# Turning the fourth layer's features on SyncE's DMA queue and its rows on GpSimd's, with buffers of their own

## The chip, the cores and the metric

The kernel runs on one core of a Trainium2 chip. The metric is the device time of one execution in microseconds (us). TensorE (PE in the profile) does the matmuls, VectorE (DVE), ScalarE (ACT) and GpSimd (POOL) the elementwise work, and DMA engines move data between the core's memory and HBM. DMAs are issued from the instruction queues of SyncE (SP) and GpSimd here; each of these queues is worked off in its order, so a DMA whose semaphore is not yet there holds up all that stand behind it.

## The reference

A graph of N = 4096 nodes with 256 features each passes through four attention layers over the same adjacency matrix. After every layer the result is added to the layer's input and each row is normalised. The third and the fourth layer are what matters here; cut to that:

```python
# layer 2: additive attention, one head
h = x @ W
e = leaky_relu((h @ a[:D])[:, None] + (h @ a[D:])[None, :], 0.01)
att = softmax(where(adj > 0, e, -1e12), axis=1)
x = layernorm(x + elu(att @ h))
# layer 3: cosine attention
Qn = (x @ Wq.T) / max(norm(x @ Wq.T, axis=-1), 1e-4)
Kn = (x @ Wk.T) / max(norm(x @ Wk.T, axis=-1), 1e-4)
att = softmax(where(adj > 0, Kn @ Qn.T, -9e15), axis=1)
x = layernorm(x + 0.5 * (att @ x) + 0.5 * x)
```

Layers are counted from 0 in the code: the "fourth layer" of this document is layer 3 of the reference. Before its attention can begin, all of its Q and K have to be there, projected from the features that layer 2 leaves behind, normalised by row and turned so that the 128 projected values lie on the partitions.

## The kernel before, in words

Nodes are worked in NB = 8 blocks of 512 rows; a block is attended against NT = 32 tiles (j = 0 to 31) of 128 nodes. The features X stay in the core's memory throughout.

**Layer 2** (`additive_one`) walks the units (b, j). For each unit ACT writes e (L451), DVE multiplies it by the edges' mask into prob (L453, three buffers), and PE adds prob times V to the block's sums (L459). The masks, one DMA of 512 KB for two tiles, are issued from SP's queue (L449, four buffers). When block b has been summed, DVE divides (L465, L467), and in the first tiles of block b + 1 it finishes block b: `add_elu`, then `layernorm_block`. So the finished features of block b are there early in block b + 1.

**The preparation of layer 3** (`Cosine.prepare`) is laid between the tiles of layer 2's last block, for the blocks n = 0 to 5; the blocks 6 and 7 are prepared inside layer 3. It has three steps for each block:

- step 0 turns the features: `block_apart` lets DVE transpose X in squares of 32 x 32 into a tile `squares` (L130, two instructions), writes it to a tile in HBM (L133, 512 KB) and reads it back in another order into xT (L135, four DMAs of 128 KB). The function `turned_apart` does this.
- step 1 projects: PE multiplies xT with both weight matrices (L852), ACT sums the squares (L857), DVE copies the result to `rows` (L858) and scales it (L863).
- step 2 turns the rows: again `turned_apart`, from `rows` through `squares` and HBM into T (L130, L133, L135).

Step 1 of block n stands behind tile j = 2 + 4n of the last block in PE's order, step 2 at j = 5 + 4n. Layer 3 reads T of block n at its tile j = 4n. Between these steps GpSimd also issues the first masks of layer 3 (L835), each behind a small copy `tick` (L91) that makes it wait for a chosen tile of layer 2.

Only PE's order is written out by hand (`manual_schedule` for PE). The orders of DVE, ACT, POOL and SP come from a scheduler, which puts an instruction where its inputs and its buffers are free. That is why the features of the blocks 0, 1 and 2 are already transposed in the course of layer 2, long before the place where the code names them.

What the steps share in the kernel before: one buffer `squares` (pool `co_once`) for features and rows alike, two buffers of xT and two of rows (pool `co_in`), and one queue for all the DMAs of the turning, GpSimd's for the blocks 0 to 5 (`eng = nc.gpsimd if b < NB - 2 else nc.sync`) and SP's for 6 and 7.

Of the kernel before, what the change touches and what calls it, by code (L numbers as in the profile page):

```python
# [9 lines left out]
FP = mybir.dt.float32  # L10
# [8 lines left out]
P = 128  # L19
D = 256  # L20
KC = D // P
QB = 4
# [6 lines left out]
def kernel(  # L29
# [27 lines left out]
    nc = tc.nc  # L57
# [4 lines left out]
    def pool(stack, name, bufs, **kw):  # L62
        return stack.enter_context(tc.tile_pool(name=name, bufs=bufs, reuse_waits="tile", **kw))
# [56 lines left out]
            copies[c](xT[:, c, :], pt)  # L120
        return xT.rearrange("p c (k i) -> p c k i", i=P)

    def turned_apart(once, dr, part, to, eng):

        B = P // QB
        squares = once.tile([P, QB, KC, P], FP, name="squares")
        for c in range(KC):
            nc.vector.transpose(squares[:, :, c, :].rearrange("p q (k n) -> p k q n", n=B),  # L130
                                part(c).rearrange("p k (q f) -> p k q f", f=B))
        far = dr.tile([QB, B, QB, KC * P], FP, name="squares_far")
        eng.dma_start(far.rearrange("a f q m -> (a f) (q m)"), squares.rearrange("p q c m -> p (q c m)"))  # L133
        for q in range(QB):
            eng.dma_start(to[q * B:(q + 1) * B], far[:, :, q, :].rearrange("a f m -> f a m"))  # L135
        return to.rearrange("p a (c m) -> p c a m", c=KC)
# [264 lines left out]
    def additive_one(w_sb, slope, tail, op, follow):  # L401
# [3 lines left out]
        with ExitStack() as lay:  # L405
# [4 lines left out]
            row = keep.tile([P, N], FP, name="row")  # L410
            zp = pool(lay, "gb_z", 3)
            sb = pool(lay, "gb_sb", 2)
            mp = pool(lay, "gb_mask", 4)
            dr = pool(lay, "gb_dram", 2, space=bass.MemoryType.DRAM)

# [6 lines left out]
                return ps.tile([P, QW], FP, name="g")  # L422

            def turn(b):
                return transposed_block(sb, bank, b)

            def project(b, xT, ks=range(QB)):
                groups = [(k, 1, bank().rearrange("p (n f) -> p n f", n=1)) for k in ks]
# [380 lines left out]
    class Cosine:  # L809
# [7 lines left out]
        def start(self):  # L817
            keep = self.stack.enter_context(tc.tile_pool(name="co_keep", bufs=1, side="right", reuse_waits="tile"))
            self.pool = self.stack.enter_context(tc.tile_pool(name="co_in", bufs=2, side="right", reuse_waits="tile"))
            self.masks = self.stack.enter_context(tc.tile_pool(name="co_mask", bufs=4, side="right", reuse_waits="tile"))  # L820
            self.mask = {}

            self.T = [keep.tile([P, QB, 2 * P], FP, name=f"T{b}") for b in range(NB)]
            self.dram = self.stack.enter_context(tc.tile_pool(name="co_dram", bufs=2, space=bass.MemoryType.DRAM))
            self.once = self.stack.enter_context(tc.tile_pool(name="co_once", bufs=1, side="right", reuse_waits="tile"))
            self.w_sb = keep.tile([P, KC, 2 * P], FP, name="w3_sb")
            load_w(self.w_sb[:, :, :P], wq3T, nc.sync)
            load_w(self.w_sb[:, :, P:], wk3T, nc.sync)
# [8 lines left out]
        def prepare(self, bank, b, step):  # L837

            in_, w_sb = self.pool, self.w_sb

            eng = nc.gpsimd if b < NB - 2 else nc.sync
            if step == 0:
                self.xT[b] = block_apart(in_, self.once, self.dram, b, eng)
            elif step == 1:
                xT = self.xT.pop(b)
                norm = in_.tile([P, QB, 2], FP, name="norm")
                rows = self.rows[b] = in_.tile([P, QB, 2, P], FP, name="rows")
                for k in range(0, QB, 2):
                    pr = bank().rearrange("p (t n f) -> p t n f", t=2, f=P)
                    for t in range(2):  # L850
                        for c in range(KC):
                            nc.tensor.matmul(pr[:, t, :, :], xT[:, c, k + t], w_sb[:, c, :],  # L852
                                             start=(c == 0), stop=(c == KC - 1))
                    for t in range(2):
                        for n in range(2):
                            sq = in_.tile([P, P], FP, name="sq")
                            nc.scalar.activation(sq, pr[:, t, n, :], AF.Square, accum_out=norm[:, k + t, n:n + 1])  # L857
                    nc.vector.tensor_copy(rows[:, k:k + 2], pr)  # L858
                v = in_.tile([P, QB * 2], FP, name="v")
                nc.vector.tensor_scalar_max(v, norm.rearrange("p k n -> p (k n)"), 1e-8)  # L860
                r = inverse_root(v, QB * 2)
                flat = rows.rearrange("p k n f -> p (k n) f")
                nc.vector.tensor_tensor(flat, flat, r.unsqueeze(2).to_broadcast([P, QB * 2, P]), OP.mult)  # L863
            else:
                rows = self.rows.pop(b)
                turned_apart(self.once, self.dram, lambda n: rows[:, :, n, :], self.T[b], eng)

    def cosine_attention(co, tail):
        MJ = co.MJ
        T = [t.rearrange("p k (n i) -> p n k i", n=2) for t in co.T]  # L870
        with ExitStack() as lay:
            sb = pool(lay, "co_sb", 3)
            yp = pool(lay, "co_y", 2)

            pa = pool(lay, "co_pa", 1, space=PSUM)
            pz = pool(lay, "co_pz", 2, space=PSUM)
            ps = pool(lay, "co_ps", 2, space=PSUM)
            ov = out.rearrange("(t p) d -> p t d", p=P)
            acc, prob, y = {}, {}, {}

            def bank():
                return ps.tile([P, QW], FP, name="g")

            def weights(b, j):
                m = b, j // MJ
                if m not in co.mask:
                    co.load_mask(*m)
                p = bank() if b and j % 2 else pz.tile([P, QW], FP, name="p")
                nc.tensor.matmul(p.rearrange("p (k i) -> p k i", k=QB), T[j // QB][:, 0, j % QB], T[b][:, 1],  # L889
                                 start=True, stop=True)  # L890

                z = prob[b, j] = sb.tile([P, QW], FP, name="prob")
                nc.scalar.activation(z, p, AF.Exp)  # L893
                nc.vector.tensor_tensor(z, z, co.mask[m][:, j % MJ, :], OP.mult)  # L894

            def sums(b, js):
                if js[0] == 0:
                    acc[b] = [pa.tile([P, D + 1], FP, name=f"acc{k}") for k in range(QB)]
                for k in range(QB):
                    for j in js:  # L900
                        nc.tensor.matmul(acc[b][k], prob[b, j][:, k * P:(k + 1) * P], X[:, j, :],  # L901
                                         start=(j == 0), stop=(j == NT - 1))

            def outputs(b, n):

                for k0 in range(0, QB, n):
                    mv = fin.tile([P, n, 2], FP, name=f"mv{n}")
                    for k in range(k0, k0 + n):
                        rden = fin.tile([P, 1], FP, name="rden1")
                        nc.vector.reciprocal(rden, acc[b][k][:, D:])  # L910
                        nc.vector.scalar_tensor_tensor(y[b][:, k, :], acc[b][k][:, :D], rden, y[b][:, k, :], OP.mult, OP.add)
                        one_row(mv, k - k0, y[b][:, k, :])
                    normalise([y[b][:, k, :] for k in range(k0, k0 + n)], mv)
                    nc.sync.dma_start(ov[:, b * QB + k0:b * QB + k0 + n, :], y[b][:, k0:k0 + n, :])

            units = [(b, j) for b in range(NB) for j in range(NT)]
            LAG = 2
            steps = {(0, j + n): (NB - 2 + b, step) for b, j in enumerate((1, 12)) for step, n in enumerate((0, 5, 8))}
            for i in range(len(units) + LAG):
                if i < len(units):  # L920
                    b, j = units[i]
                    weights(b, j)
                    if (b, j) == (0, 1):
                        tail(bank)
                    if (b, j) in steps:
                        co.prepare(bank, *steps[b, j])
                if i >= LAG:
                    b, j = units[i - LAG]
                    if j == NT - 8:
                        y[b] = yp.tile([P, QB, D], FP, name="y")  # L930
                        nc.scalar.mul(y[b], X[:, b * QB:(b + 1) * QB, :D], 1.5)

                    if i < len(units):
                        sums(b, [j])
                    elif i > len(units):
                        sums(b, [j - 1, j])
                    if j == NT - 1:
                        outputs(b, QB if b < NB - 1 else 2)
# [88 lines left out]
```

## Time and profile before

| | us |
|---|---|
| median of three runs (2909.53 to 2911.84) | 2911.56 |
| the profiled execution's own time | 2912.43 |
| its span (first to last instruction) | 2910.7 |
| PE busy | 2889.4 |
| DVE busy | 1954.2 |
| ACT busy | 1655.3 |
| POOL busy | 965.2 |

Of the DMAs that turn features and rows, POOL's queue issues 12 writes (L133) and 48 reads (L135), SP's queue 4 and 16. The span is the time that the profile can divide; the execution's own time is 1.73 us longer. In the rows shown below, a line such as "PE L852 MATMUL acc<-w_sb,xT" is an instruction at line 852 that reads w_sb and xT and writes acc; "[7.90 <-DMA xT<-squares_far]" says that its engine sat idle for 7.90 us before it, until that DMA had landed. A float32 matmul shows as two records, so a tile of layer 2 (four matmuls) has 8 and a projection of a block (eight) has 16. In the tables by stretch of time the last columns are the clock granted to PE (1.00 is full), the mean busy share of the DMA engines, and GB/s.

### The profile page before, as it was taken

How to read it: one execution, taken by the hardware profiler on the slowest of the kernel's cores; microseconds unless marked ns; L12 is line 12 of the kernel's file. 1: busy time of each engine (PE TensorE's matmuls, PEld its weight loads, DVE VectorE, ACT ScalarE, POOL GpSimd, SP SyncE). 2: the span in 40 equal slices, each digit the busy share in tenths (PEclk: the TensorE clock that was granted, in tenths of full speed). 3: DMA queues.
4: the chain of work that ended last, by engine and by line, in shares of the span. 5: the costliest groups of instructions: out<-in, count | busy, mean ns of one | idle time of the engine just before them, and what ended most of it. 6: DMA issues, size and time to landing. Idle time of an engine off the chain costs nothing.

```text
span 2910.7 us, 50256 instructions
## 1 busy us (share of the span) xinstructions
PE 2889.4 (99%) x20141; PEld 1553.4 (53%) x20141; DVE 1954.2 (67%) x2541; ACT 1655.3 (57%) x2589; POOL 965.2 (33%) x735
## 2 busy tenths in 40 slices
PE   9999999999999999999999999999998999999998
PEld 4333333333643333333333358888887777777776
DVE  8899999998677777777777765655666423333333
ACT  7899999997356666666666654444443222222222
POOL 0010010100068989989889860000012000000000
PEclk9999999999999999999999999999999999999999
DMA  7566667665068989889889875655566434434341
GB/s 205 103 138 137 139 139 145 135 129 90 1 134 193 185 186 193 183 187 192 182 189 191 182 171 133 178 163 150 154 185 168 87 58 58 58 58 58 58 58 29
DMA packets 214061, 391.72 MB, mean 135 GB/s; under 512 B 16338, under 2 KB 94146, under 8 KB 212931
## 3 DMA queue, kind: packets, MB, share of 16 engines
q0 software_dynamic: 106336, 190.35, 40.2%
q1 hardware_dynamic: 107216, 197.88, 22.3%
q8 instruction: 158, 2.59, 0.3%
q14 instruction: 77, 0.62, 0.1%
q10 hardware_dynamic: 274, 0.26, 0.0%
HBM read 325.46 MB, written 29.43 MB: 122 GB/s over the span
## 4 chain that ended last, share of the span: by engine, by line
PE 98%; DMA 1%; DVE 1%; ACT 0%; issue 0%; POOL 0%; DVEq 0%; POOLq 0%
PE acc L293 23%; PE acc L901 15%; PE acc L678 15%; PE p L645 15%; PE acc L459 8%; PE g L459 7%; PE p L889 4%; PE g L889 3%; PE g L572 2%; PE g L196 1%; PE pv L587 1%; PE acc L196 1%; PE g L118 1%; PE acc L852 1%; DMA squares_far<-squares 1%; PE g L305 0%
## 5 line engine op out<-in xcount | busy, mean ns | idle before, releaser
L657 DVE TENSOR_TENSOR prob<-p,mask 128x1024 f32<-128x1024 f32 x512 | 624.1, 1223 | 209.5 <-ACT p L647 203.8
L647 ACT ACTIVATE p<-p,shift 128x1024 f32<-128x1024 f32 x512 | 556.2, 1088 | 325.2 <-PE p L645 324.4
L293 PE MATMUL acc<-prob,V 128*32 128x512 f32 x6144 | 664.0, 592 | 1.2 <-DVE prob L283 1.2
L664 POOL TENSOR_TENSOR den<-den,prob 128x1024 f32<-128x1024 f32 x248 | 626.9, 2528 | 72.6 <-DVE prob L657 64.7
L280 ACT ACTIVATE prob<-row,dst 128x512 f32<-128x512 f32 x1020 | 633.1, 712 | 0.1
L283 DVE SCALAR_TENSOR_TENSOR prob<-prob,mask 128x2048 f32<-128x2048 f32 x256 | 582.5, 2286 | 24.2 <-ACT prob L280 20.7
L645 PE MATMUL p<-qT,kT 64*64 64x512 f32 x4096 | 532.3, 590 | 0.8 <-DVE prob L657 0.8
L678 PE MATMUL acc<-prob,V 64*64 64x512 f32 x4096 | 531.5, 589 | 0.0
L901 PE MATMUL acc<-X,prob 128*128 128x257 f32 x2048 | 485.5, 380 | 0.0
L901 PEld LDWEIGHTS acc<-X,prob 128*128 128x128 f32 x2048 | 388.6, 190 | 162.8 <-issue 112.9
L894 DVE TENSOR_TENSOR prob<-prob,mask 128x512 f32<-128x512 f32 x256 | 176.2, 690 | 409.3 <-ACT prob L893 408.1
L293 PEld LDWEIGHTS acc<-prob,V 128*32 128x32 f32 x6144 | 197.3, 110 | 453.1 <-issue 433.6
L451 ACT ACTIVATE e<-row,dst 128x512 f32<-128x512 f32 x256 | 184.0, 721 | 241.8 <-DVE prob L453 212.6
L678 PEld LDWEIGHTS acc<-prob,V 64*64 64x64 f32 x4096 | 155.9, 133 | 285.4 <-issue 278.1
L645 PEld LDWEIGHTS p<-qT,kT 64*64 64x64 f32 x4096 | 154.4, 133 | 277.3 <-issue 261.5
L453 DVE SCALAR_TENSOR_TENSOR prob<-e,mask 128x512 f32<-128x512 f32 x256 | 177.6, 695 | 173.4 <-PE acc L459 93.9
L91 POOL COPY tick<-prob 128x1 f32<-128x1 f32 x35 | 40.0, 1144 | 645.9 <-DVE prob L283 644.8
L835 POOL DMA_DIRECT2D mask<-in_adjT x64 | 47.6, 743 | 582.2 <-DVE prob L894 505.3
L670 POOL DMA_DIRECT2D den<-prob x240 | 231.6, 965 | 14.7 <-DVE prob L657 7.5
L893 ACT ACTIVATE prob<-p 128x512 f32<-128x512 f32 x144 | 85.7, 596 | 257.0 <-PE p L889 243.0
L459 PE MATMUL acc<-V,prob 128*128 128x257 f32 x1024 | 225.1, 380 | 0.0
L459 PE MATMUL g<-V,prob 128*128 128x257 f32 x1024 | 224.1, 380 | 0.0
(160 smaller groups left out, 1965.6 us busy)
## 6 DMA issues: line engine op xcount, KB each, us to landing
mask<-in_adjT SPq DMA_DIRECT2D x256, 512.0 KB
den<-prob POOLq DMA_DIRECT2D x240, 512.0 KB, 5.3
mask<-edges SPq DMA_DIRECT2D x256, 128.0 KB
mask<-in_adjT POOLq DMA_DIRECT2D x64, 512.0 KB, 5.7
edges<-in_adj POOLq DMA_DIRECT2D x32, 512.0 KB, 10.0
den<-prob SPq DMA_DIRECT2D x16, 512.0 KB
row<-far SPq DMA_DIRECT2D x7, 1024.0 KB
squares_far<-squares POOLq DMA_DIRECT2D x12, 512.0 KB, 4.0
```

The lines of the kernel that those rows point to most:

```text
L280: nc.scalar.activation(z[:, h, :], r, AF.Relu, bias=-1.0, scale=dst[:, j, h:h + 1])
L283: nc.vector.scalar_tensor_tensor(z, z, 1.0, mask[m][:, j % MJ, :].unsqueeze(1).to_broadcast([P, H, QW]), OP.add, OP.mult)
L293: nc.tensor.matmul(acc[b][h * G:(h + 1) * G, n, :], part, prob[b, j][:, h, :], start=(j == 0), stop=(j == NT - 1))
L459: nc.tensor.matmul(acc[b][k][:, :D + 1], prob[b, j][:, k * P:(k + 1) * P], V[:, j, :], start=(j == 0), stop=(j == NT - 1))
L645: nc.tensor.matmul(p[c * d:(c + 1) * d, r, :], kT[half, c, j * d:(j + 1) * d], qT[half, c, cols], start=True, stop=True)
L647: nc.scalar.activation(p, p, AF.Exp, bias=shift)
L657: nc.vector.tensor_tensor(z, p, mask[m][:, j % MJ, :].unsqueeze(1).to_broadcast([P, KC, QW]), OP.mult)
L664: nc.gpsimd.tensor_tensor(to, to, flat, OP.add)
L670: nc.gpsimd.dma_start(to, flat, accum_op=OP.add)
L678: nc.tensor.matmul(acc[b][c][r * d:(r + 1) * d, :], V[half, j, r * d:(r + 1) * d], prob[b, j][half, r, :], start=(j == 0), stop=(j == NH - 1))
L889: nc.tensor.matmul(p.rearrange("p (k i) -> p k i", k=QB), T[j // QB][:, 0, j % QB], T[b][:, 1], start=True, stop=True)
L901: nc.tensor.matmul(acc[b][k], prob[b, j][:, k * P:(k + 1) * P], X[:, j, :], start=(j == 0), stop=(j == NT - 1))
```

## The change

Features and rows each get what they shared before.

- The features' step gets three pools that live with layer 2 itself (`gb_turn` with three buffers of xT, `gb_squares` with one, `gb_far` in HBM), handed over as `follow.turning`; inside layer 3, for the blocks 6 and 7, it gets `co_turn` (two), `co_squares` and `co_turn_far`. Layer 2's own transposed blocks use `gb_turn` too, instead of two buffers in `gb_sb`.
- The features' DMAs (step 0) are issued from SP's queue for all blocks. The rows' DMAs (step 2) stay on GpSimd's queue for the blocks 0 to 5 and on SP's for 6 and 7.
- The rows keep `co_once` for their squares; `rows` itself moves there too and so has one buffer instead of two.

```diff
-    def turned_apart(once, dr, part, to, eng):
+    def turned_apart(squares, far, part, to, eng):
         B = P // QB
-        squares = once.tile([P, QB, KC, P], FP, name="squares")
+        squares = squares.tile([P, QB, KC, P], FP, name="squares")
+        far = far.tile([QB, B, QB, KC * P], FP, name="far")
         for c in range(KC):
             nc.vector.transpose(...)
-        far = dr.tile([QB, B, QB, KC * P], FP, name="squares_far")
         eng.dma_start(far..., squares...)
         for q in range(QB):
             eng.dma_start(to[q * B:(q + 1) * B], far[:, :, q, :]...)
...
             sb = pool(lay, "gb_sb", 2)
+            xp = pool(lay, "gb_turn", 3)
+            sq = pool(lay, "gb_squares", 1)
+            far = pool(lay, "gb_far", 2, space=bass.MemoryType.DRAM)
+            follow.turning = xp, sq, far
...
-                return transposed_block(sb, bank, b)
+                return transposed_block(xp, bank, b)
...
-            self.dram = ... tile_pool(name="co_dram", bufs=2, DRAM)
             self.once = ... tile_pool(name="co_once", bufs=1, ...)
+            self.far = ... tile_pool(name="co_far", bufs=2, DRAM)
...
-            eng = nc.gpsimd if b < NB - 2 else nc.sync
             if step == 0:
-                self.xT[b] = block_apart(in_, self.once, self.dram, b, eng)
+                self.xT[b] = block_apart(*self.turning, b, nc.sync)
             elif step == 1:
...
-                rows = self.rows[b] = in_.tile([P, QB, 2, P], FP, name="rows")
+                rows = self.rows[b] = self.once.tile([P, QB, 2, P], FP, name="rows")
...
-                turned_apart(self.once, self.dram, lambda n: rows[:, :, n, :], self.T[b], eng)
+                turned_apart(self.once, self.far, lambda n: rows[:, :, n, :], self.T[b],
+                             nc.gpsimd if b < NB - 2 else nc.sync)
...
+            co.turning = (pool(lay, "co_turn", 2), pool(lay, "co_squares", 1),
+                          pool(lay, "co_turn_far", 2, space=bass.MemoryType.DRAM))
```

More of the change, by code (lines that the diff above doesn't have):

```diff
@@ L823, in start @@
             self.T = [keep.tile([P, QB, 2 * P], FP, name=f"T{b}") for b in range(NB)]
-            self.dram = self.stack.enter_context(tc.tile_pool(name="co_dram", bufs=2, space=bass.MemoryType.DRAM))
             self.once = self.stack.enter_context(tc.tile_pool(name="co_once", bufs=1, side="right", reuse_waits="tile"))
+            self.far = self.stack.enter_context(tc.tile_pool(name="co_far", bufs=2, space=bass.MemoryType.DRAM))
             self.w_sb = keep.tile([P, KC, 2 * P], FP, name="w3_sb")
```

## The prediction

> **What bounds the kernel now.** I read the page's engine shares and its chain first, then PE's waits, then PE in order of time around the longest wait, and last the queue that this wait hangs on.
>
> The page, engine shares:
>
> ```profile
> PE 2889.4 (99%) x20141; PEld 1553.4 (53%) x20141; DVE 1954.2 (67%) x2541; ACT 1655.3 (57%) x2589; POOL 965.2 (33%) x735
> ```
>
> The list of waits, in us: total, times, longest:
>
> ```profile
> PE acc L852 <- DMA xT<-squares_far: 8.7, 2, 7.9
> ...
> POOL xT L135 <- PE acc L852: 218.6, 3, 212.6
> ```
>
> PE is busy for 2889.4 of 2910.7 us, so all its idle time is 21.3 us. 8.7 of them are two waits of the projections (L852) for turned features; the rest lies at the start of the kernel and behind the last matmul. A change in the turning can give back these 8.7 us and what hangs on them, and no more. The third row is POOL standing 212.6 us before the reads of the third block's features: both xT buffers are full until PE's first projection.
>
> PE in order of time, over layer 2's last block:
>
> ```profile
> 2173.38 7.10 PE L459 MATMUL g<-V,prob 128*128 128x257 f32 x32
> 2181.28 3.69 PE L852 MATMUL acc<-w_sb,xT 128*128 128x256 f32 x16 [0.79 <-DMA xT<-squares_far]
> 2184.81 7.10 PE L459 MATMUL g<-V,prob 128*128 128x257 f32 x32
> 2199.81 6.55 PE L852 MATMUL acc<-w_sb,xT 128*128 128x256 f32 x16 [7.90 <-DMA xT<-squares_far]
> 2206.20 7.10 PE L459 MATMUL g<-V,prob 128*128 128x257 f32 x32
> 2213.13 3.62 PE L852 MATMUL acc<-w_sb,xT 128*128 128x256 f32 x16
> 2216.59 15.78 PE L459 MATMUL g<-V,prob 128*128 128x257 f32 x72
> 2232.20 2.98 PE L889 MATMUL p<-T 128*128 128x512 f32 x6
> ```
>
> The fourth projection waits 0.79 us, the fifth 7.90. The fifth also takes 6.55 us where the same 16 records take 3.62 elsewhere. Stretches of 5 us show why: the granted clock, third column from the end.
>
> ```profile
> 2190.00:2195.00 5.00, 1.91 (x9) 1.33 (x7) 2.74 (x5) 2.16 (x3) 0.67 (x2) 1.00 0.95 304
> 2195.00:2200.00 5.00, 0.19 (x1) 0.22 (x2) 0.11 (x1) 0.00 (x0) 2.07 (x4) 0.54 0.84 267
> 2200.00:2205.00 5.00, 5.00 (x12) 3.98 (x13) 1.53 (x3) 1.14 (x8) 2.74 (x5) 0.50 0.48 152
> 2205.00:2210.00 5.00, 5.00 (x23) 4.32 (x22) 2.70 (x9) 2.28 (x11) 2.18 (x4) 0.94 0.41 138
> ```
>
> PE came out of the long wait at half clock. POOL in order of time shows what the features waited for:
>
> ```profile
> 2183.00 2.20 POOL L135 DMA_DIRECT2D T<-squares_far  x4 [4.71 <-DMA squares_far<-squares]
> 2185.20 0.57 POOL L133 DMA_DIRECT2D squares_far<-squares  x1
> 2194.33 2.18 POOL L135 DMA_DIRECT2D xT<-squares_far  x4 [8.56 <-DMA squares_far<-squares]
> 2196.50 0.57 POOL L133 DMA_DIRECT2D squares_far<-squares  x1
> 2200.80 2.19 POOL L135 DMA_DIRECT2D T<-squares_far  x4 [3.73 <-DMA squares_far<-squares]
> ```
>
> Rows and features alternate in one queue through one squares buffer. The fifth block's features were written at 2185.20, behind the T reads of the third block's rows; the write took 8.56 us to land, and the reads began at 2194.33. PE wanted them at 2191.9.
>
> [...] 0.54 and 0.50 after 7.90 us of idling, no drop after 0.79. [...] the four reads at 2194.33 and the write at 2196.50 moved together. [...]
>
> **The change part by part.**
>
> *Features 0 to 5: squares and buffers.* In the order that the changed kernel builds, DVE transposes the features of all six blocks as soon as layer 2 has normalised them, in blocks 1 to 6; before, only 0, 1 and 2. The first three are read into three xT buffers at once; those of 3, 4 and 5 are written to HBM early and read only when a projection frees a buffer. Cost on DVE: the same two instructions for each block, 1.30 us, three pairs moved from the last block into blocks 4 to 6. They lie beside PE: DVE is busy for 32.45 us of the 55.51 us from 1921.86, which holds such a pair, and PE is busy for all 55.51. Without this cover 1.3 us each, 3.9.
>
> *The reads of 3, 4 and 5.* In SP's order each group of four stands behind a projection: xT of block 3 waits for projection 0. By the trace this ends at 2152.4; the read then has until projection 3. Three periods of 32 + 16 records, 6.94 + 3.45 = 10.39 us, less that projection itself, are 27.7 us. Before, reads took 2.8 to 7.5 us to land (median 3.7). So the waits of 0.79 and 7.90 go, and with the long one the slow clock: 6.55 - 3.45 = 3.10 us (3.45 is a projection in the chain). Sum: -0.79 - 7.90 - 3.10 = **-11.79 us**. Cross-check: the last block from 2143.91 to 2232.20 takes 88.29 us; undisturbed it is 55.51 us for its 32 x 8 = 256 records of L459 (the stretch of the block from 1921.86) and 6 x 3.45 = 20.70 for the projections, together 76.21; the difference is 12.08. I take 11.8, and 12.1 as the most.
>
> *SP's queue.* 6 writes and 24 reads move from POOL to SP. Issue time on SP: 6 x 0.34 + 24 x 0.43 = 12.4 us over some 400 us, about 2.1 us for a block. What stands behind them are layer 2's masks, one in 3.47 us (two tiles of 8 records, 2 x 1.735). At the early three boundaries one mask stands between the write and the first reads, so a read's wait for the write delays the next mask only where the write takes more than about 2 + 3.5 us, measured from the mask's turn. Writes from SP landed in 2.7 to 6.6 us (squares issued at 2237.58, 2259.45, 2264.11, 2289.99; their reads at 2240.29, 2262.10, 2267.96, 2296.63), from POOL in 2.9 to 8.6. Masks run three pairs ahead, 10.4 us; with some 4 us to land, an estimate from those writes, 6.4 stay for DVE, and prob's three buffers hide two more tiles, 3.5, from PE. A delay of 3 us is hidden; unhidden it would be up to 3 us three times. In the last block the mask before each group of reads is released by tile 5 + 4n, while projection n is on PE, and the next by tile 7 + 4n, after it. The reads wait inside that gap: no mask is late. Cost 0; bounds 0 to 9 us.
>
> *POOL's queue.* It keeps six writes and 24 reads of rows, 4 tick copies or masks between them. Per block 0.56 + 2.20 us of issue and one landing, 4.0 us median, about 6.8 of 10.39 us; before, the rows and the features of two blocks shared that time. T of block n gets no later, and layer 3 reads T5 only at its tile 20. Gain 0 by itself, since nothing on PE waits for T before.
>
> *One rows buffer, one squares buffer for rows.* DVE writes and reads both in its own order, so rows cannot wait for another engine. Squares wait for the rows' write of the block before: it has 10.39 us against 4.0 median, 8.6 at worst. Cover: DVE's wait of 2.73 us at 2216.86 left PE without a gap. Cost 0; bound 3 us.
>
> *Blocks 6 and 7.* Their features get their own squares, and PE's projection of block 7 moves one tile earlier. Its features are transposed before the rows of block 6, not after. PE has no wait in layer 3 before; its end is set by PE and the last outputs, untouched. Cost 0, bounds -0.3 to +1.
>
> Against the profiled execution: 2912.43 - 11.79 = 2900.6 (span 2898.9). It lies 0.87 above the median of the runs; from the median, 2911.56 - 11.79 = **2899.8 us**, 0.40% less.
>
> **The rivals.** *A, the wait only shrinks.* DMA share stays near 1 in the last block (six rows through HBM, three features, four masks for layer 3), a rows write holds DVE's transposes for 5.5 us as once before, prob comes late, and PE idles some 3 us, without the slow clock or with part of it. For it speaks that the 4 masks took 5.8 to 13.2 us to land there; against it that three 512 KB writes have left the stretch. Time: 2899.8 + 3 to 6, 2903 to 2906.
>
> *B, the wait moves.* The same, long enough for the clock to fall: one stall of 5 to 8 us plus 3.1 gives 2908 to 2911, no change. Against it: only one DMA chain for each 10.39 us is left on either queue.
>
> *C, slower.* A read on SP waits for its write with a mask behind it, at the three early boundaries. To lose 5.8 us net (0.2%) it must take 17.6 back, 5.9 at each boundary, so 2.8 us idle and 3.1 of slow clock. The write must then take 2 + 3.5 + 6.4 + 3.5 + 2.8 = about 18 us to land; the most seen is 8.6. Time at that point 2917.4. Nothing in the trace comes near.
>
> **How the numbers follow.** Changes of less than 0.2% (5.8 us) are about what a measurement of this kernel can't tell from none. The forecast, all 11.8 us or nearly (2898 to 2902), 0.78; A 0.12, nearly all of it still faster by more than 0.2%; B 0.05; C 0.05. Faster by over 0.2% (below 2905.7): 0.89; within: 0.06; slower: 0.05. The range goes from 2897 (12.1 us off the median, and the spread of the runs, 2.3 us) to 2905.5, which takes in most of A and the bounds of the unknown costs save their sum.
>
> **What would show it.** In the changed profile PE's wait for xT is gone, the granted clock stays 1.00 from 2140 to the end of layer 2, and layer 3's first matmul stands near 2220.4 instead of 2232.20. SP shows its L135 reads early, with no DVE or PE wait on a mask of layer 2. POOL's 212.6 us wait for a projection is gone. The prediction is wrong if PE's idle time outside start and end is more than 2 us, above all before L459 (prob late) or L852, or if a block of layer 2 before the last takes longer than 55.5 us.

## The result, and the profile after

The changed kernel takes 2899.5 us (median of six runs, 2898.84 to 2901.93), the kernel before 2911.7 (six runs, 2909.53 to 2913.19). The ratio is 0.996 with a 95% interval of 0.9948 to 0.9973: faster by 0.4%, or 12.2 us. The prediction was 2899.8. The profiled execution of the changed kernel took 2899.22 us, its span 2897.4.

The changed kernel's lines lie lower in the code: the masks' DMA is L454, e L456, prob L458, prob times V L464, the projection L855, its copy to rows L861, the turning L131 (transposes), L133 (write) and L135 (reads), layer 3's first matmul L896.

The page of the changed kernel, engine shares:

```profile
PE 2885.2 (100%) x20141; PEld 1552.3 (54%) x20141; DVE 1954.7 (67%) x2541; ACT 1654.8 (57%) x2589; POOL 948.8 (33%) x705
```

The changed kernel's list of PE's waits, complete (us in total, times, longest):

```profile
PE acc L293 <- DVE prob L283: 1.1, 1, 1.1
PE acc L358 <- DVE X L80: 1.1, 1, 1.1
PE p L650 <- DVE prob L662: 0.8, 1, 0.8
PE acc L196 <- DVE xT L120: 0.5, 1, 0.5
PE g L118 <- DMA X<-in_x: 0.4, 1, 0.4
PE g L577 <- ACT xT L120: 0.4, 1, 0.4
```

No projection waits for xT any more, and no matmul of layer 2 waits for prob. PE's idle time is 2897.4 - 2885.2 = 12.2 us instead of 21.3, and PE's busy time is 4.2 us less for the same 20141 records, most of it because none of them runs at half clock: up to 2890, behind which PE does nothing more, the granted clock is 1.00 in every stretch of 5 us, where before it was 0.50 from 2200 to 2205. PE in order of time over layer 2's last block, in the changed kernel:

```profile
2142.61 5.37 PE L464 MATMUL g<-V,prob 128*128 128x257 f32 x24
2147.81 3.62 PE L855 MATMUL acc<-w_sb,xT 128*128 128x256 f32 x16
...
2189.37 3.62 PE L855 MATMUL acc<-w_sb,xT 128*128 128x256 f32 x16
2192.83 7.10 PE L464 MATMUL g<-V,prob 128*128 128x257 f32 x32
2199.76 3.62 PE L855 MATMUL acc<-w_sb,xT 128*128 128x256 f32 x16
2203.22 15.78 PE L464 MATMUL g<-V,prob 128*128 128x257 f32 x72
2218.83 2.98 PE L896 MATMUL p<-T 128*128 128x512 f32 x6
```

All six projections have the same 3.62 us and no bracket with a wait behind them. From the block's first matmul to layer 3's first it is 2218.83 - 2142.61 = 76.22 us. The same two matmuls of the kernel before stand at 2143.75 and 2232.20, 88.45 us apart. This length, the **block length** from here on, is the measure for all kernels below: it leaves out the start of the kernel, which differs by some 2 us between the executions profiled for the table of experiments below. The difference is 12.23 us, and the medians differ by 12.2, so nothing was gained or lost elsewhere. Layer 3 shows the same: from its first matmul to the end of the span 2910.7 - 2232.20 = 678.5 us before and 2897.4 - 2218.83 = 678.6 after.

Stretches of 5 us of the changed kernel, where PE stood still and then ran at half clock before (PE, PEld, DVE, ACT and POOL busy, then granted clock, busy share of the DMA engines, which as the profile counts it can pass 1, and GB/s):

```profile
2190.00:2195.00 5.00, 5.00 (x25) 4.38 (x24) 2.74 (x7) 3.49 (x18) 0.56 (x1) 1.00 1.13 239
2195.00:2200.00 5.00, 5.00 (x25) 4.38 (x24) 4.22 (x10) 1.86 (x4) 0.99 (x2) 1.00 0.88 286
2200.00:2205.00 5.00, 5.00 (x25) 4.40 (x24) 2.34 (x5) 3.50 (x18) 1.75 (x4) 1.00 0.96 266
```

PE is full and the clock is 1.00, while the DMA engines are at least as busy as before. The amount of traffic was not the limit.

What moved shows on DVE. The kernel before, DVE in order of time, the transposes of the rows of block 0 and then of the features of blocks 3, 4 and 5:

```profile
2158.55 1.29 DVE L130 STREAM_TRANSPOSE squares<-rows 128x512 f32<-128x512 f32 x2
...
2165.49 1.30 DVE L130 STREAM_TRANSPOSE squares<-X 128x512 f32<-128x512 f32 x2 [1.66 <-DMA squares_far<-squares]
...
2182.45 1.30 DVE L130 STREAM_TRANSPOSE squares<-X 128x512 f32<-128x512 f32 x2 [1.15 <-DMA squares_far<-squares]
...
2200.61 1.30 DVE L130 STREAM_TRANSPOSE squares<-X 128x512 f32<-128x512 f32 x2 [5.50 <-DMA squares_far<-squares]
```

The same three transposes of features in the changed kernel (the first of the two instructions of each):

```profile
1991.91 0.71 DVE L131 STREAM_TRANSPOSE squares<-X 128x512 f32<-128x512 f32 x1
...
2047.41 0.71 DVE L131 STREAM_TRANSPOSE squares<-X 128x512 f32<-128x512 f32 x1
...
2102.93 0.71 DVE L131 STREAM_TRANSPOSE squares<-X 128x512 f32<-128x512 f32 x1
```

They stand 98 to 174 us earlier, and wait for no landing. The order in which the code names the work explains the old place: the rows of block n are named behind tile 5 + 4n of the last block, the features of block n + 3 behind tile 6 + 4n. With one buffer of squares for both, the features of block 3 get it only after the rows of block 0, which have to be projected first.

The reads on SP's queue in the last block, changed kernel, SP in order of time:

```profile
2151.46 1.79 SPq L135 DMA_DIRECT2D xT<-far  x4
2157.34 3.09 SPq L454 DMA_DIRECT2D mask<-in_adjT  x2
2161.85 1.89 SPq L135 DMA_DIRECT2D xT<-far  x4
...
2172.24 2.35 SPq L135 DMA_DIRECT2D xT<-far  x4
```

xT of block 5 is asked for at 2172.24, and its projection is due at 2199.76. On POOL's queue the longest wait is now one for a rows write, changed kernel, POOL in order of time:

```profile
2168.53 0.57 POOL L133 DMA_DIRECT2D far<-squares  x1 [0.80 <-DVE squares L131]
...
2178.36 2.20 POOL L135 DMA_DIRECT2D T<-far  x4 [9.27 <-DMA far<-squares]
```

The write issued at 2168.53 was there 9.83 us later. DVE's next transpose of rows waited 0.77 us for it, and PE did not notice.

### The profile page after: what moved, and what is told of

It reads as the page before. It is cut to its first block, busy times and chain, and to the rows that moved or that the text cites. A ratio compares the mean times of both kernels' runs of the same rounds, so it can differ in the third digit from the quotient of the medians.

```text
span 2897.4 us, 50242 instructions
## 1 busy us (share of the span) xinstructions
PE 2885.2 (100%) x20141; PEld 1552.3 (54%) x20141; DVE 1954.7 (67%) x2541; ACT 1654.8 (57%) x2589; POOL 948.8 (33%) x705
## 4 chain that ended last, share of the span: by engine, by line
PE 99%; DVE 1%; ACT 0%; DMA 0%; issue 0%; SPq 0%; DVEq 0%
PE acc L293 23%; PE acc L683 15%; PE acc L908 15%; PE p L650 15%; PE acc L464 8%; PE g L464 8%; PE p L896 4%; PE g L896 3%; PE g L577 2%; PE g L196 1%; PE pv L592 1%; PE acc L855 1%; PE g L118 1%; PE acc L196 1%; PE g L305 0%; PE p L720 0%
## 5 line engine op out<-in xcount | busy, mean ns | idle before, releaser
L283 DVE SCALAR_TENSOR_TENSOR prob<-prob,mask 128x2048 f32<-128x2048 f32 x256 | 582.7, 2288 | 24.1 <-ACT prob L280 21.5
L456 ACT ACTIVATE e<-row,dst 128x512 f32<-128x512 f32 x256 | 183.9, 721 | 245.8 <-DVE prob L458 216.6
L458 DVE SCALAR_TENSOR_TENSOR prob<-e,mask 128x512 f32<-128x512 f32 x256 | 177.5, 694 | 169.1 <-PE acc L464 91.4
L464 PE MATMUL acc<-V,prob 128*128 128x257 f32 x1024 | 225.1, 380 | 0.0
L464 PE MATMUL g<-V,prob 128*128 128x257 f32 x1024 | 223.7, 380 | 0.0
```

What stands on the lines that cost most here:

```text
L283: nc.vector.scalar_tensor_tensor(z, z, 1.0, mask[m][:, j % MJ, :].unsqueeze(1).to_broadcast([P, H, QW]), OP.add, OP.mult)
L464: nc.tensor.matmul(acc[b][k][:, :D + 1], prob[b, j][:, k * P:(k + 1) * P], V[:, j, :], start=(j == 0), stop=(j == NT - 1))
```

## The experiments

The change has three parts that can be had one by one: **the queue** (features issued from SP instead of POOL), **the squares** (a buffer of squares for the features alone), and **the third xT buffer**. A fourth, one buffer of `rows` instead of two, stayed in all the kernels below, as did the new layout of the pools. The features' own tiles in HBM (`gb_far`) belong to that layout, so no run says whether squares of their own would do the same without them. Each kernel is the changed one with the edits shown:

```diff
# queue taken back: features on POOL's queue for blocks 0 to 5
-                self.xT[b] = block_apart(*self.turning, b, nc.sync)
+                self.xT[b] = block_apart(*self.turning, b, nc.gpsimd if b < NB - 2 else nc.sync)
# squares taken back: rows use the features' squares
-                turned_apart(self.once, self.far, lambda n: rows[:, :, n, :], self.T[b],
+                turned_apart(self.turning[1], self.far, lambda n: rows[:, :, n, :], self.T[b],
# third xT buffer taken back
-            xp = pool(lay, "gb_turn", 3)
+            xp = pool(lay, "gb_turn", 2)
```

The theory was the prediction's: features of blocks 3 to 5 come late because they share squares and queue with the rows. The rivals were that one of the three parts alone does it, and that the rest of the change does (rows buffer, layout, a new order by the scheduler). The results together, in us; the ratio is to the kernel before, with its 95% interval:

| kernel | queue | squares | 3 xT | median | ratio | block length |
|---|---|---|---|---|---|---|
| before | | | | 2911.7 | 1 | 88.45 |
| none of the three | - | - | - | 2911.97 | 1.0001 (0.9993 to 1.0010) | 88.34 |
| third xT alone | - | - | yes | 2911.5 | 0.9998 (0.9989 to 1.0006) | 88.09 |
| queue alone | yes | - | - | 2907.96 | 0.9990 (0.9983 to 0.9997) | 83.37 |
| all but squares | yes | - | yes | 2909.26 | 0.9989 (0.9983 to 0.9996) | 83.71 |
| squares alone | - | yes | - | 2902.67 | 0.9970 (0.9959 to 0.9981) | 79.12 |
| all but third xT | yes | yes | - | 2901.32 | 0.9961 (0.9947 to 0.9975) | 77.32 |
| all but queue | - | yes | yes | 2900.04 | 0.9956 (0.9941 to 0.9971) | 77.16 |
| changed | yes | yes | yes | 2899.5 | 0.9960 (0.9948 to 0.9973) | 76.22 |

### None of the three

All three edits above. Expected:

> The changed kernel with three of its parts undone: features on GpSimd's queue, one squares buffer for rows and features, two buffers of xT. What stays is the single rows buffer and the places in memory. All theories: the wait of the fifth projection is back, 2911.7 us within 2. A time near 2899.5 would mean that the rows buffer or the layout did it.

Measured 2911.97 us, and the old waits are back. PE in order of time:

```profile
2199.22 6.10 PE L855 MATMUL acc<-w_sb,xT 128*128 128x256 f32 x16 [7.32 <-DMA xT<-far]
```

The fifth projection waits 7.32 us and runs slow, as in the kernel before. So the single `rows` buffer and the pools' layout do nothing by themselves, and the three parts hold the whole gain.

### The third xT buffer alone

The first two edits. Expected:

> Only the third buffer of xT. Theories Squares and Queue: nothing gained, 2908 to 2913. Theory xT: 2898 to 2902.

Measured 2911.5 us. PE in order of time:

```profile
2198.09 5.85 PE L855 MATMUL acc<-w_sb,xT 128*128 128x256 f32 x16 [7.96 <-DMA xT<-far]
```

A place to read into is no help while what is to be read has not been written.

### The queue alone

The last two edits. Expected:

> Only the features' queue is changed to SP. Theory Squares (the late features come from rows and features taking turns in one squares buffer, with a landing of 4 to 9 us at each turn): DVE still transposes the features of blocks 3 to 5 after the rows of 0 to 2, part of the wait stays, 2903 to 2909. Theory Queue (they come from standing behind the rows' DMAs in POOL's queue): PE's waits for xT are gone, 2898 to 2901.

Measured 2907.96 us, some 3.7 less than before; the block is 5.1 us shorter. The time lies in the range for shared squares and far above that for the queue. PE's wait for xT is gone, and another stands in its place. DVE in order of time, with the features of blocks 4 and 5, queue alone:

```profile
2177.94 1.31 DVE L131 STREAM_TRANSPOSE squares<-X 128x512 f32<-128x512 f32 x2 [2.80 <-DMA far<-squares]
2179.80 0.68 DVE L458 SCALAR_TENSOR_TENSOR prob<-e,mask 128x512 f32<-128x512 f32 x1
...
2192.67 1.30 DVE L131 STREAM_TRANSPOSE squares<-X 128x512 f32<-128x512 f32 x2 [4.72 <-DMA far<-squares]
2194.53 0.68 DVE L458 SCALAR_TENSOR_TENSOR prob<-e,mask 128x512 f32<-128x512 f32 x1
```

And PE in order of time, same kernel:

```profile
2180.54 3.37 PE L464 MATMUL g<-V,prob 128*128 128x257 f32 x8 [2.17 <-DVE prob L458]
2183.71 3.97 PE L855 MATMUL acc<-w_sb,xT 128*128 128x256 f32 x16
...
2195.27 2.00 PE L464 MATMUL g<-V,prob 128*128 128x257 f32 x8 [2.38 <-DVE prob L458]
```

This is a chain to read step by step. DVE stands before the transpose until the rows' write has landed and the squares are free. The next prob is queued behind it on DVE and ends at 2180.48 and 2195.21. PE takes it up at 2180.54 and 2195.27. The wait has moved from PE's projections to DVE and from there to prob.

### All but the squares

The second edit alone. Expected:

> The changed kernel with one squares buffer for both; SP's queue and three xT stay. Theory Squares: features 3 to 5 are transposed after the rows of 0 to 2 again, 2902 to 2909. Theory Queue: 2898 to 2901.

Measured 2909.26 us, just above the range for shared squares. The two waits for prob are 2.25 and 2.61 us, and DVE waits 11.2 us in all for the squares. Two of the three parts of the change bring only a fifth of its gain by the medians (2.4 of 12.2 us), and under two fifths by the block length (4.7 of 12.2; the profiled execution was one of the fastest of this kernel, 2907.09 us).

### The squares alone

The first and the third edit. Expected:

> Only the squares are changed: features have their own, all on POOL's queue, two buffers of xT. Theory Squares: features 3 to 5 are written to HBM in blocks 4 to 6 of layer 2, the reads alone stand in POOL's queue, no wait of PE for xT, 2898 to 2901. Theory Queue: the reads stand behind the rows' landings, 2905 to 2912. Theory xT (two buffers let a read begin too late): 2905 to 2912 as well.

Measured 2902.67 us: three quarters of the gain by one pool, although the features are still issued from POOL's queue. The features of blocks 3 to 5 are transposed in blocks 4 to 6 of layer 2, the last of them at 2105. It lay outside what was expected, and the remaining 2.9 us of block length are these waits of PE, squares alone, in order of time:

```profile
2186.43 2.00 PE L464 MATMUL g<-V,prob 128*128 128x257 f32 x8 [0.96 <-DVE prob L458]
2189.21 3.74 PE L464 MATMUL g<-V,prob 128*128 128x257 f32 x16 [0.78 <-DVE prob L458]
```

1.74 us in all, with half a microsecond of small gaps beside them, and two stretches of 32 records that take 7.41 us instead of 7.10. DVE does not wait for any landing here. What differs is the order that the scheduler wrote: between the third projection's work and the fourth's, ACT has three e in its order and DVE three prob, where the changed kernel has four of each. So prob runs out while ACT and DVE do the projection's squares and copies. That the order is the cause was read from the two instruction orders, and no kernel was run with the other order alone.

### All but the queue, and all but the third xT buffer

The first edit alone. Expected:

> The changed kernel with the features back on GpSimd's queue; own squares and three xT stay. Theory Squares: 2898 to 2901, no wait of PE for xT. Theory Queue: the wait is back in part, 2904 to 2912.

The third edit alone. Expected:

> The changed kernel with two buffers of xT. Theories Squares and Queue: a read issued at the end of a projection has one period and one run of tiles (10.4 + 6.9 = 17.3 us) to land in 3 to 8 us, so 2898 to 2901. Theory xT: PE waits for xT again, above 2903.

Measured 2900.04 and 2901.32 us; the second lies 0.3 us above its range. Neither has a wait for xT, and the second has one of 0.7 us for prob. Their intervals and that of the changed kernel overlap, so the runs do not tell how the last two or three microseconds fall to the queue and the third buffer; either of them on top of the squares is enough for nearly all of the gain.

### Rows on SP's queue too

This tests the mechanism of the prediction's slower rival: a read on SP that waits for its write, with masks behind it. The edit:

```diff
                 turned_apart(self.once, self.far, lambda n: rows[:, :, n, :], self.T[b],
-                             nc.gpsimd if b < NB - 2 else nc.sync)
+                             nc.sync)
```

Expected:

> The changed kernel with the rows of blocks 0 to 5 on SP's queue too. If a read that waits for its write's landing holds back layer 2's masks behind it by more than they run ahead (the mechanism of rival C), PE waits for prob in the last block and the time is 2902 to 2915. If the lead of three masks and prob's buffers hide it, 2898 to 2901.

Measured 2910.45 us, ratio 0.9993 (0.9985 to 1.0002): the gain is gone. Its waits of SP in the last block, then of DVE in the same stretch:

```profile
SPq L135 <- DMA far<-squares: 21.5, 6, 5.8
```

```profile
DVE prob L458 <- DMA mask<-in_adjT: 7.1, 2, 5.8
```

And PE in order of time, the same kernel:

```profile
2195.15 3.80 PE L464 MATMUL g<-V,prob 128*128 128x257 f32 x8 [7.25 <-DVE prob L458]
2198.74 4.68 PE L855 MATMUL acc<-w_sb,xT 128*128 128x256 f32 x16
```

Six times SP's sequencer stood before reads until a write had landed, 21.5 us in all and 5.8 at most. A mask of layer 2 was issued only at 2189.05, behind reads of rows at 2186.33 and of xT, prob waited 5.8 us for it, and PE 7.25 us for prob, with the slow clock after it. So it matters that the rows stayed on the other queue. The rival's mechanism exists, though not in the place and not through one slow write of 18 us, as the prediction priced it: in the last block, with twice as many writes in the queue, six shorter waits are enough. The changed kernel has no case of it. On SP its reads wait at most 3.1 us for a write, and no mask is late.

### The price of a stall of PE

The prediction took 3.10 us for the slow clock behind the long wait. Its own trace had shown two waits: the clock fell to 0.54 and 0.50 after 7.90 us of idling and stayed at 1.00 after 0.79. What a stall of a length between these brings, that trace does not show; the expectations below set one with a fall of the clock against one without. To measure it apart from the turning, a matmul of 128 x 128 that is not used was put behind n copies on GpSimd in the fourth block of layer 2, which has no wait otherwise:

```diff
+                        if (b, j) == (3, 10):
+                            late = keep.tile([P, QW], FP, name="late")
+                            for _ in range(n):
+                                nc.gpsimd.tensor_copy(late, prob[b, j])
+                            spare = pa.tile([P, QW], FP, name="acc0")
+                            nc.tensor.matmul(spare[:, :P], late[:, :P], ident, start=True, stop=True)
```

n = 5. Expected:

> The changed kernel with one wait put into PE's order in block 3 of layer 2, after tile 10: a small matmul (128 columns, its result unused) that reads a tile written by 5 copies in a row on GpSimd. PE idles some 1 to 3 us. [...] granted clock stays 1.00 around it, and the time is 2899.5 plus the idle time. If every wait cost some 3 us more, the tiles behind it would take 8 records in about 3.5 us.

n = 12. Expected:

> The same with 12 copies, for an idle time of some 6 to 10 us. [...] the time is 2899.5 plus the idle time plus 2 to 4 us. Without it: plus the idle time alone.

n = 8. Expected:

> The changed kernel with one extra matmul behind 8 copies on GpSimd in layer 2's fourth block; its result is not used. By 5 copies (0.31 us idle) and 12 copies (5.06 us), 0.68 us for each copy, PE should stand 2.4 us. Theory 1, [...] no fall, the time is that of 5 copies, 2900.8, plus 2.1 us, 2902.9, and all executions lie together. Theory 2, [...] (it fell behind 2.17 us of idling in the kernel with only the queue moved, and not behind 2.38 in the same execution): it falls in some executions and costs 1.7 us in these, so the times spread from 2902.5 to some 2905, with a median of 2903 to 2904.5.

n = 10. Expected:

> As with 8 copies, but 10: PE should stand 3.7 us. Theory 1, [...] the clock falls in every execution and stays low for one step of 3.4 us of work, 1.7 us lost; 2900.8 + 3.4 + 1.7 = 2905.9. Theory 2, [...] it falls in nearly all executions too, [...] so the loss is 0 to 1.7 us where the low step begins before PE is back; 2904.2 to 2905.9.

| n | idle of PE, us | low clock, us | median, us (lowest to highest) |
|---|---|---|---|
| 5 | 0.31 | none | 2900.79 (2899.91 to 2901.00) |
| 8 | 2.35 | 3.4, in the profiled execution | 2902.14 (2901.63 to 2907.38) |
| 10 | 3.71 | 3.4 | 2905.38 (2903.67 to 2907.55) |
| 12 | 5.06 | 3.4 | 2907.39 (2905.74 to 2911.23) |

The stalls came out shorter than first expected for 5 and 12 copies. From 5 to 12 copies the idle time grows by 5.06 - 0.31 = 4.75 us and the median by 6.60, 1.85 more; from 5 to 10 copies by 3.40 and 4.59, 1.19 more. The medians take in the start of the kernel, the block itself does not. From its first matmul to that of the next block it takes 56.32, 60.04, 61.40 and 62.75 us in the profiled executions with 5, 8, 10 and 12 copies; of the last three each is 1.68 us longer than its idle time explains. That is half of 3.4 us of work at half clock. So in these three executions a stall cost its own length and then some 1.7 us for the 3.4 us of low clock in which PE worked.

With 8 copies the idle time of 2.35 us was followed by the low clock too, in the profiled execution. Stretches of 1 us of it, columns as above:

```profile
1944.00:1945.00 1.00, 0.00 (x0) 0.00 (x0) 0.00 (x0) 0.00 (x0) 0.92 (x2) 1.00 0.73 219
1945.00:1946.00 1.00, 0.29 (x2) 0.29 (x3) 0.31 (x1) 0.00 (x0) 0.62 (x1) 1.00 1.06 422
1946.00:1947.00 1.00, 1.00 (x7) 0.89 (x7) 0.38 (x1) 0.58 (x1) 0.00 (x0) 1.00 0.71 291
1947.00:1948.00 1.00, 1.00 (x4) 0.81 (x3) 0.00 (x0) 0.14 (x1) 0.00 (x0) 0.50 0.61 90
```

PE was back at 1945.71 and the clock fell at 1947.0, more than a microsecond into the work. That execution took 2907.38 us, of which another 2.1 us are a wait at the start of the kernel. The other four lie at 2901.63 to 2902.50, at or a little under what was expected without a fall. The profiled execution speaks against the first theory, no fall with 8 copies, and for the second, a fall in some executions; that the four others had none is inferred from their times, since they have no trace. For 10 copies the two theories gave nearly the same time, and the run does not tell them apart.

## Why the prediction was right, point by point

**The sum.** -0.79 - 7.90 - 3.10 = -11.79 us stood against 12.2 measured. The cross-check on the last block gave 76.21 us undisturbed, and the block took 76.22. The sum lacks 0.44 us against the 12.23 of the block. From start to start the rows of the kernel before give all of it. A run of 32 records takes 7.10 us, yet the next starts 6.93 after it where nothing waits, so each of the two waits also costs 0.17 of lost overlap. The slow projection takes 2206.20 - 2199.81 = 6.39 instead of 3.46, so 2.93: the 3.10 set a length (6.55) against a distance of starts (3.45) and took in one of the two 0.17. What the sum lacks is the other 0.17 and 0.27 of small gaps, in the run of 7.30 us at 2162.80 and in the fourth projection's 3.69. The cross-check's 12.08 is 0.16 too little, since it began at 2143.91, the end of the run before, and not at 2143.75. Against the profiled execution the forecast was 2900.6 and the time 2899.22. Of the 1.4 us between them 1.1 lie ahead of the block: it began at 2142.61 instead of 2143.75, from a start of the kernel that went 0.9 us faster in this execution. For that reason too layer 3 began at 2218.83 and not at 2220.4.

**Features early, DVE beside PE.** Right. The transposes run in blocks 4 to 6 and PE has no gap there. POOL's wait of 212.6 us for a projection is gone, as forecast.

**What the features waited for.** The prediction wrote that "rows and features alternate in one queue through one squares buffer", and left it open which of the two holds them up. The runs decide: the buffer. With squares of their own and the old queue the features come early (2902.67 us); with the new queue and the old squares they do not, and DVE's waits for the squares go into prob. The reason is the order in which a shared buffer is filled: in the kernel before, the transposes of the features of blocks 3 to 5 come behind rows of the last block, 98 to 174 us after the changed kernel has done them. Since the change took both away, the prediction was right without having to know which; a forecast that gave the queue alone the whole gain would have been some 8 us too low.

**POOL's queue, "gain 0 by itself".** Right as it was meant, for the rows: PE's lists of waits have none for T, before or after. As a whole the move of the queue is worth little too: without it the time is 2900.04, and the intervals overlap. Only beside the shared squares does the queue change anything to speak of, and then by a third.

**SP's queue, cost 0.** Right for this change. PE waits for no prob in the changed kernel. The upper bound of 9 us was not idle caution: with the rows' reads on SP as well, 10.3 us of block length are lost (86.55 against 76.22).

**One squares buffer for rows, cost 0, bound 3.** Right in its effect, narrow in its margin. A write was taken to land in 4.0 us, 8.6 at worst, against a period of 10.39. In the changed kernel one took 9.83 us. DVE waited 1.4 us in all, and nothing of it reached PE.

**One `rows` buffer; blocks 6 and 7.** Right: the control with none of the three parts equals the kernel before, and layer 3 is as long as before to within 0.1 us.

**The slow clock, 3.10 us.** Right in this place, because the wait of 7.90 us was gone altogether. As a price it is not a constant: some 1.7 us behind 2.2 to 5.1 us of idling, 2.2 to 3.0 us behind 7.3 to 8.0 (the projection after the wait, or the tile and the projection after it, against their length elsewhere).

**The rivals.** A, prob late through a rows write that holds DVE's transposes, is just what the queue alone brings, with stalls of 2.17 and 2.38 us. The changed kernel escapes it by the buffer, not by the shorter queue. Its price of "3 us, without the slow clock or with part of it" was on the low side, as the first stall of 2.17 us cost about 1.8 us more behind it. B, the same with a long stall, was not seen. C was seen only with the rows on SP too, and there its stall of 7.25 us came in the last block.

## What to carry to other kernels

When a transfer is late, follow it back past its queue to the buffer it is filled from, and ask in which order that buffer is handed out: a one-deep buffer shared by an early chain and a late one ties the early one to the late one's landings, and another queue or more room at the far end does not untie them. Price each part of a change of several parts by what the others leave in place; here squares alone brought 9 us, the queue alone under 4, the third buffer alone nothing. For the clock, add to a stall of PE of 2 to 5 us some 1.7 us, and to one of 7 or 8 up to 3: an estimate from the 1.68 us lost behind 2.35, 3.71 and 5.06 us of idling here, and the 2.2 to 3.0 behind 7.3 to 8.0.

## What the runs showed of the hardware

The low clock lasted 3.4 us in some of these executions, and twice or three times as long in others. Summed from stretches of 1 us, each stretch at clock c counting for (1 - c) / 0.5 of its length, it lasted 3.4 us behind idling of 2.17 us (queue alone), 2.25 (all but squares), 2.35 (8 copies), 3.71 (10) and 5.06 (12); 6.8 us behind 7.32 (none of the three); and 10.2 us behind 7.25 (rows on SP too), 7.90 (the kernel before) and 7.96 (third xT alone). In these runs the length of the idling alone does not tell whether the clock falls: the low clock came after 2.17, 2.25 and 2.35 us of idling, while 2.38 and 2.61 us in the same two executions as the first two brought none. The prediction's "no drop after 0.79" stands.

Queue alone, stretches of 1 us around its first stall, columns as above:

```profile
2180.00:2181.00 1.00, 0.46 (x2) 0.43 (x3) 0.91 (x4) 0.82 (x3) 0.61 (x2) 1.00 0.87 262
2181.00:2182.00 1.00, 1.00 (x5) 0.73 (x4) 0.95 (x2) 0.24 (x1) 0.76 (x1) 0.51 0.99 397
...
2184.00:2185.00 1.00, 1.00 (x5) 0.83 (x5) 1.00 (x3) 0.42 (x1) 0.00 (x0) 0.79 0.91 145
```

The clock falls at 2181.0, 0.5 us after PE took up its work at 2180.54, and is back at 2184.4. With 8 copies it fell 1.3 us after PE was back. What decides whether a stall of 2 to 3 us brings the low clock, these runs do not show.

The second finding is the landing time of a 512 KB write from the core to HBM on POOL's queue while the DMA engines' share is near 1. From its issue to that of the reads behind it, one took 9.83 us in the changed kernel (share 1.05 over that time) and one 11.57 in the kernel with all but the third xT buffer (2189.79 to 2201.36, share 1.06), where the median before was 4.0. Of 10.39 us for each block, the rows' chain has no slack left there.
